# A gated recurrence with residual on one core: the order of the first loads, x of steps 8 to 15 by transposing load, and the last plain step by inner chunks

## The chip, the cores and the metric

The kernel runs on one core of a Trainium2 chip. The metric is the device time of one execution in microseconds, and the median of several runs is compared. A profile of one execution gives the times of the single instructions.

## What is computed

A GRU runs over 128 steps for a batch of 64. Input and state have 512 elements each. The kernel returns x plus the states of all steps, in float32:

```python
def step(h, inp):
    x_t, prop = inp
    comb = jnp.concatenate([x_t, h], axis=-1)
    z = jax.nn.sigmoid(comb @ Wz + bz)
    r = jax.nn.sigmoid(comb @ Wr + br)
    comb2 = jnp.concatenate([x_t, r * h], axis=-1)
    h_cand = jnp.tanh(comb2 @ Wh + bh)
    h_new = (1.0 - z) * h + z * h_cand
    h_next = jnp.where(prop, jnp.tanh(h_new @ Wp + bp), h_new)
    return (h_next, h_new)
```

`prop` is true at every fourth step, except at the last one. The upper 512 rows of each weight matrix meet x (tile `wx`, all three gates), the lower 512 meet the state (tiles `wh`). The recurrence is serial: a step's gates need the state of the step before. The part with x is known ahead and can be computed at any time before its step.

## The kernel before

**Layout.** The 512 columns are cut into two halves, and the 64 rows of the batch stand twice on the 128 partitions, once for each half. A product of one gate is four chunks of 128 input elements (k = 0 to 3, worked in the order 0, 2, 1, 3), each for both column halves: `product`, L195, one unit of the filler queue described below. The input of a product has to be transposed, with input elements on the partitions. `turn` (L204) does this on TensorE for the 16-bit words of the float32 values: four multiplies per 128 columns, and a copy out of PSUM.

**The parts with x.** Steps are taken in groups of four (g = t // 4). For steps 0 to 7 and for the last group they are plain products (`plain`, L410; `plain_last`): 12 units for a step, three gates times four chunks. All groups between go through `batch`: a nested scheme with seven products in place of eight at two levels, which needs sums of blocks of x (on POOL, `sum_raw12`, `sum_s12` and the like) and sums of blocks of `wx`. Part of the weight sums overwrite `wx` itself (`sum_outer_1`, L313, chunks 0 and 2; `sum_inner_1`, L322), so they come after the last plain product that reads those blocks, which is that of step 7.

**The order.** It is written out by hand; every engine works through its instructions in the order of the program. In a step TensorE does the R products from `hT`, the Z products, the turning of r*h, then filler units, the products of the candidate, filler units, and the turning of the new state. ACT does the sigmoids and tanh and part of the copies out of PSUM, DVE the elementwise work and other copies. `queue` holds the units of the parts with x, and `fill(n)` puts n of them where TensorE would wait for ACT and DVE. `read_out` appends the copies and sums that take a finished filler result out of PSUM; `seed` puts the x part of the next step into the accumulator, on ACT.

**x transposed.** There are two ways to it. `turn_x` (L235) turns one step's x on TensorE, with two copies on ACT: this is done for steps 0 to 15, from the tiles `xr` (groups 0 and 1) and `early` (groups 2 and 3). From group 4 on, `words_x` (L247, POOL) splits the words into a tile `xw`, `planes_x` (L257) issues a transposing load on SP from `xw` into `xv`, and `join_x` (L267, ACT) puts the words together in `xT`. `xw` and `xv` have one buffer each, `xT` two. The `early` tiles are two of the three buffers that later hold results of the batches (`mb`).

**The start.** SP asks for both halves of x of steps 0 and 1 (L109), then z's and the candidate's `wx`; ACT asks for r's `wx`, the initial state and three biases. Then SP goes on with the recurrent weights of r, x of steps 2 and 3, the bias of the propagation, the recurrent weights of z and of the candidate, and x of groups 1, 2 and 3 with `wp` between (L127 to L145). TensorE begins with multiplies of zeros (`idle`, L171, called from L595), turns x of steps 0 and 1 between them, and takes the plain products of steps 0 and 1 gate by gate before step 0 starts at L621.

Of the kernel before, what the change touches and what calls it, by code (L numbers as in the profile page):

```python
# [11 lines left out]
U16 = mybir.dt.uint16  # L12
# [5 lines left out]
def kernel(  # L18
# [29 lines left out]
    nc = tc.nc  # L48
    B, T, D = x.shape
    H = h0.shape[1]  # L50
    P = 128
    S = 2
    N = H // S
    C = N // P
    K = D // P
    Q4 = 4
    CHUNK = 4
    FIRST = 2
    LAST = T // Q4 - 1
    R, Z, H_ = range(3)  # L60
# [21 lines left out]
    wx = const.tile([P, K, 3, H], F32, name="wx")  # L82
# [5 lines left out]
    gates_in = (Wr, Wz, Wh)  # L88
    def load_x(tile_, t0, n, j=0):
        for s in range(S):  # L90
            nc.sync.dma_start(  # L91
                out=tile_[s * B : (s + 1) * B, j : j + n, :], in_=x[:, t0 : t0 + n, ts(s, N)]
            )

    def load_w(wt, w, k0, k1, eng):
        eng.dma_start(
            out=wt[:, k0:k1, :],
            in_=w[k0 * P : k1 * P, :].rearrange("(k p) n -> p k n", p=P),
        )

    xr = {}

    def new_xr(g):
        xr[g] = xrp.tile([P, Q4, N], F32, tag="xr", name=f"xr_{g}")
# [1 line left out]
    h_init = two.tile([P, N], F32, tag="h", name="h_init")  # L106
    bias_in = const.tile([P, 4, N], F32, name="bias")
    new_xr(0)
    load_x(xr[0], 0, 2)  # L109
    for i in range(3):  # L110
        for k in (0, 2):
            load_w(wx[:, :, i, :], gates_in[i], k, k + 2, nc.scalar if i == R else nc.sync)

    def load_bias(i, eng):
        for s in range(S):
# [22 lines left out]
    early = {}  # L138
# [25 lines left out]
    def cut(ps):  # L164
        return ps.rearrange("p (c n) -> p c n", c=C)
# [29 lines left out]
    def product(ps, lT, w, k, start=False):  # L195
        s0, c0 = divmod(k, C)
        products(ps, lT[:, c0, ts(s0, B)], lambda s: w[:, k, ts(s, N)], start)

    ORDER = [s * C + c for c in range(C) for s in range(S)]

    def copy(eng, dst, src):
        (eng.copy if eng is nc.scalar else eng.tensor_copy)(dst, src)  # L202

    def turn(src, dst, c, name, eng):  # L204


        pt = turn_ps[c][:, :P].bitcast(BF16).rearrange("p (w n) -> p w n", w=2)
        for s in range(S):
            words = src[:, c * P + s * B : c * P + (s + 1) * B].bitcast(BF16)
            for w in range(2):  # L210
                nc.tensor.transpose(  # L211
                    pt[s * B : (s + 1) * B, w, :],
                    words.rearrange("p (n w) -> p w n", w=2)[:, w, :],
                    ident16,
                )
        copy(
            eng,
            dst[:, c, :].bitcast(U16).rearrange("p (n w) -> p n w", w=2),
            pt.bitcast(U16).rearrange("p w n -> p n w"),
        )  # L220

    def new_T(tag, name):
        return two.tile([P, C, P], F32, tag=tag, name=name)
# [3 lines left out]
    xs = {}  # L227
    xw = {}
    xv = {}

    def new_xT(g):
        if g not in xT:
            xT[g] = xtp.tile([P, Q4, C, P], F32, tag="xT", name=f"xT_{g}")

    def turn_x(t, eng=nc.scalar):  # L235
        g, i = divmod(t, Q4)
        new_xT(g)
        src = xr[g] if g < 2 else early[g]
        for c in range(C):
            turn(src[:, i, :], xT[g][:, i], c, f"xT_{t}", eng)  # L240
# [6 lines left out]
    def words_x(g, i):  # L247

        if g * Q4 >= T:
            return  # L250
        if g not in xw:
            xw[g] = one.tile([P, Q4, 2, N], U16, tag="xw", name=f"xw_{g}")
        nc.gpsimd.tensor_copy(
            xw[g][:, i], xs[g][:, i, :].bitcast(U16).rearrange("p (n w) -> p w n", w=2)
        )

    def planes_x(g):  # L257

        if g * Q4 >= T:
            return  # L260
        xv[g] = one.tile([P, Q4, 2, C, P], U16, tag="xv", name=f"xv_{g}")
        nc.sync.dma_start_transpose(
            out=xv[g].rearrange("p t w c n -> p (t w c) n"),
            in_=xw[g].rearrange("p t w n -> p (t w n)"),
        )

    def join_x(g, i):  # L267

        if g * Q4 >= T:
            return  # L270
        new_xT(g)
        nc.scalar.copy(  # L272
            xT[g][:, i].bitcast(U16).rearrange("p c (n w) -> p w c n", w=2), xv[g][:, i]
        )


    def outer(kb, nb, ka):

        return wx[:, ka * C + kb, :, :].rearrange("p g (s n u) -> p n s g u", s=S, n=C)[:, nb]
# [12 lines left out]
    def inner(i, ka, na):  # L292
        return OPERAND[i](ka)[:, :, :, ts(na, P // 2)]
# [19 lines left out]
    def sum_outer_1():  # L313
        for ka in range(S):
            nc.vector.tensor_sub(outer(0, 1, ka), outer(0, 1, ka), outer(0, 0, ka))
# [6 lines left out]
    def sum_inner_1(i, eng):  # L322
        eng.tensor_sub(inner(i, 0, 1), inner(i, 0, 1), inner(i, 0, 0))
# [23 lines left out]
    def sum_s12(g):  # L347
        v = xT[g]
        o = sx[g, "o12"] = one.tile([P, 2, 2, P], F32, tag="o12", name=f"o12_{g}")
        nc.gpsimd.tensor_add(o[:, 0], v[:, 2:4, 0, :], v[:, 2:4, 1, :])  # L350
        nc.gpsimd.tensor_sub(o[:, 1], o[:, 0], v[:, 0:2, 0, :])
        s = sx[g, 56] = one.tile([P, 4, 2, B], F32, tag="s56", name=f"s56_{g}")
        four([s[:, n] for n in range(4)], o[:, :, 0], o[:, :, 1])
# [31 lines left out]
    def new_cp(q):  # L385
        if q not in cp:
            cp[q] = one.tile([P, C, 2, 3, P], F32, tag=f"cp{q % 2}", name=f"cp_{q}")
            for b in range(2):
                G[2 * q + b] = cp[q][:, :, b]

    def seed(i, t):
        if t < T:
            nc.scalar.copy(cut(slots[i]), G[t][:, :, i, :])  # L393
# [12 lines left out]
    def read_out():  # L406
        while pending:
            pending.pop(0)()

    def plain(t):  # L410

        first, second = scratch[:2] if t % 2 == 0 else scratch[2:]
        regions = (first[:, :N], first[:, N:], second[:, :N])
        g, i = divmod(t, Q4)

        def end():
            new_cp(t // 2)
            nc.vector.tensor_add(  # L418
                G[t][:, :, 0:2, :],
                first.rearrange("p (g c n) -> p c g n", g=2, c=C),  # L420
                bias[:, :, 0:2, :],
            )
            nc.vector.tensor_add(G[t][:, :, 2, :], cut(second[:, :N]), bias[:, :, 2, :])

        units = [
            lambda e=e, k=k: product(
                regions[e], xT[g][:, i], wx[:, :, e, :], k, k == ORDER[0] and e != Z
            )
            for e in range(3)
            for k in ORDER  # L430
        ]
        return [(u, None) for u in units[:-1]] + [(units[-1], end)]

# [187 lines left out]
    for t in range(T):  # L621
        g, j = divmod(t, Q4)
        prop = j == CHUNK - 1 and t < T - 1
        last = t == T - 1
        pair, u = divmod(t - 3, 8)
# [22 lines left out]
            assert len(queue) == 7  # L648

        def join(n):  # L650
            if pair >= 0 and u in (5, 6):
                join_x(even + 2, 2 * (u - 5) + n)
            elif pair >= 1 and u in (1, 3):
                join_x(odd, u - 1 + n)


        for k in ORDER:
            product(slots[R], hT, wh[R], k)
        if t < 6:
            turn_x((2, 5, 8, 11, 13, 15)[t])  # L660
        read_out()
        if u == 0 and pair >= 1 and odd - 2 < LAST:
            outer_u2(odd - 2)
        if t == 3:
            sum_s12(FIRST)
            for i in (1, 2, 3):
                sum_inner_1(i, nc.vector)
        rh = two.tile([P, N], F32, tag="rh", name=f"rh_{t}")
        for c in range(C):
            nc.scalar.activation(act_ps[c], slots[R][:, ts(c, P)], AF.Sigmoid)  # L670
# [30 lines left out]
        if t == 0:  # L701
            sum_outer()
            for i in (6, 7, 4):
                sum_inner(i, nc.gpsimd)
                sum_inner_1(i, nc.gpsimd)
        if not thin:
            fill(places[0])
        if t < 3:
            turn_x((3, 6, 9)[t])


        for k in ORDER:
# [12 lines left out]
            nc.vector.tensor_add(h_new[:, ts(c, P)], pc, keep[:, ts(c, P)])  # L725
        if t < T - 2:
            seed(H_, t + 1)
        read_out()
        fill(places[0] if thin else 5 if places[1] > 6 else 4)
        h = h_new  # L730
# [5 lines left out]
        fill(places[2] if thin else places[1] - 6)  # L736
        if t == 2:
            sum_outer_1()
        if prop:
            for k in ORDER:  # L740
                product(slot_p, hT, wp, k)
            read_out()
            h = two.tile([P, N], F32, tag="hprop", name=f"hprop_{t}")
            for c in range(C):
                nc.scalar.activation(h[:, ts(c, P)], slot_p[:, ts(c, P)], AF.Tanh)
            fill(behind[0] if thin else places[2] - 2)
            hT = new_T("hT", f"hpT_{t}")
            for c in range(C):
                turn(h, hT, c, f"hpT_{t}", (nc.vector, nc.scalar)[c])
            fill(behind[1] if thin else 2)  # L750
        if t < 5:
            turn_x((4, 7, 10, 12, 14)[t])


        if pair >= 0:
# [51 lines left out]
        n = 0  # L807
        if t >= T - CHUNK:
            n = {T - 2: 3, T - 1: 1}.get(t, 0)
        elif j == Q4 - 1:  # L810
            n = 4
        if n:
            for s in range(S):
                eng = nc.scalar if last and s else nc.sync
                eng.dma_start(
                    out=out[:, t - n + 1 : t + 1, ts(s, N)],
                    in_=xr[g][s * B : (s + 1) * B, j - n + 1 : j + 1, :],
# [52 lines left out]
```

## Time and profile before

| What | Value |
|---|---|
| Median of 3 runs | 1340.38 us (1339.74 to 1340.52) |
| The profiled execution: its own time, its span | 1341.68 us, 1339.9 us |
| TensorE matmul busy | 1326.0 us (99%) |
| TensorE weight load busy | 1109.8 us (83%) |
| DVE, ACT, POOL busy | 702.1 us (52%), 627.3 us (47%), 910.8 us (68%) |
| Moved by DMA | 76.74 MB, mean 57 GB/s |

The chain of work that ended last, followed back through the whole run, is 98% TensorE. By line it is L186, the products, with L211, the turning, at 5%. Busy time of an engine counts instructions that overlap, so a busy TensorE is not one at its peak. In the rows below, a group of instructions is named by line, engine and operation, and by the tile that it writes and those that it reads; "x8" is the number of instructions merged into a row. In square brackets stands the idle time of the engine before it and what ended it.

### The profile page before, as it was taken

What the parts mean: (1) busy time and instruction counts of PE and PEld (TensorE: products, weight loads), DVE (VectorE), ACT (ScalarE), POOL (GpSimd) and SP (SyncE); (2) the same over time, 40 slices, a digit from 0 to 9 for tenths busy, and PEclk for the clock granted to TensorE, in tenths of its full rate; (3) what the DMA queues carried; (4) which work ended last, traced back from release to release, by engine and by line L of the source; (5) the groups of instructions that cost most, each with busy time, mean ns of one, the idle gap of its engine ahead of it and who ended that gap; (6) DMA issues with size and microseconds to landing.
All of it is one profiled execution on the core that took longest, in us unless ns stands there. A gap on an engine that the chain in (4) does not pass through costs nothing.

```text
span 1339.9 us, 37622 instructions
## 1 busy us (share of the span) xinstructions
PE 1326.0 (99%) x15352; PEld 1109.8 (83%) x15352; DVE 702.1 (52%) x1867; ACT 627.3 (47%) x1851; POOL 910.8 (68%) x1110
## 2 busy tenths in 40 slices
PE   8999999999999999999999999999999999999998
PEld 5678888888888888888888888888888888888765
DVE  3355555555555555555555555555555555555444
ACT  1244545454554445445445544545445454554433
POOL 3448776787767777776787767777677777767500
PEclk8999999999999999999999999999999999999999
DMA  9211213122221212213212231223212222131210
GB/s 269 50 33 33 64 44 79 39 49 49 64 65 33 65 38 59 64 33 67 59 36 64 49 80 33 49 48 65 64 33 65 45 53 64 34 72 40 91 32 17
DMA packets 115500, 76.74 MB, mean 57 GB/s; under 512 B 61824, under 2 KB 110592, under 8 KB 115328
## 3 DMA queue, kind: packets, MB, share of 16 engines
q1 hardware_dynamic: 114064, 72.70, 23.5%
q8 instruction: 121, 1.98, 0.6%
q10 hardware_dynamic: 1264, 1.64, 0.5%
q14 instruction: 51, 0.42, 0.1%
HBM read 42.86 MB, written 16.78 MB: 45 GB/s over the span
## 4 chain that ended last, share of the span: by engine, by line
PE 98%; DMA 1%; DVE 0%; issue 0%; ACT 0%; SPq 0%; DVEq 0%; ACTq 0%
PE rc L186 33%; PE zp L186 20%; PE scratch_q L186 11%; PE scratch_r L186 11%; PE scratch_x L186 11%; PE scratch_a L186 6%; PE turn L211 5%; DMA xr<-in_x_dram 1%; ACT xT L202 0%; PE zp L174 0%; PE rc L174 0%; DVE turn L720 0%; SPq L91 0%; DVE h L725 0%; DVE xr L723 0%
## 5 line engine op out<-in xcount | busy, mean ns | idle before, releaser
L186 PE MATMUL rc<-wh,rhT 128*64 128x256 f32 x2048 | 245.9, 379 | 0.0
L186 PE MATMUL zp<-wh,hT 128*64 128x256 f32 x1536 | 204.3, 379 | 0.0
L186 PEld LDWEIGHTS rc<-wh,rhT 128*64 128x64 f32 x2048 | 167.6, 137 | 40.9
L542 POOL TENSOR_TENSOR cp<-mb,mb 128x768 f32<-128x768 f32 x72 | 130.9, 1818 | 102.1 <-ACT rc L393 54.5
L186 PE MATMUL rc<-wh,hT 128*64 128x256 f32 x1536 | 186.2, 383 | 0.3
L802 POOL TENSOR_TENSOR xr<-xr,h 128x256 f32<-128x256 f32 x127 | 92.8, 731 | 112.0 <-DVE h L725 111.0
L186 PEld LDWEIGHTS rc<-wh,hT 128*64 128x64 f32 x1536 | 121.1, 137 | 36.4 <-issue 9.7
L542 POOL TENSOR_TENSOR cp<-mb 128x768 f32<-128x768 f32 x44 | 79.9, 1817 | 99.3 <-ACT rc L393 98.1
L720 DVE TENSOR_TENSOR turn<-turn,z 128x128 f32<-128x128 f32 x256 | 75.4, 295 | 128.3 <-ACT turn L719 126.7
L186 PEld LDWEIGHTS zp<-wh,hT 128*64 128x64 f32 x1536 | 118.6, 137 | 25.0
L202 DVE COPY rhT<-turn 128x256 uint16<-128x256 uint16 x256 | 97.7, 420 | 69.9 <-PE turn L211 68.9
L670 ACT ACTIVATE turn<-rc 128x128 f32<-128x128 f32 x256 | 55.4, 261 | 163.2 <-issue 110.2
L202 ACT COPY hT<-turn 128x256 uint16<-128x256 uint16 x127 | 47.3, 373 | 168.6 <-DVE hT L202 128.0
L542 POOL TENSOR_TENSOR mb<-mb,mb 128x768 f32<-128x768 f32 x58 | 105.5, 1819 | 10.5 <-DVE mb L515 10.5
L393 ACT COPY rc<-cp 128x256 f32<-128x256 f32 x256 | 96.4, 376 | 19.5 <-DVE cp L418 8.0
L719 ACT ACTIVATE turn<-rc 128x128 f32<-128x128 f32 x256 | 55.2, 260 | 107.0 <-PE rc L186 105.9
L513 DVE TENSOR_TENSOR mb<-scratch_r,cq 128x384 f32<-128x384 f32 x102 | 56.7, 556 | 90.5 <-ACT cq L512 90.5
L506 DVE TENSOR_TENSOR cx<-scratch_r,cx 128x384 f32<-128x384 f32 x102 | 56.7, 556 | 86.8 <-ACT cx L504 86.8
L689 ACT ACTIVATE z<-zp 128x256 f32<-128x256 f32 x128 | 49.2, 384 | 95.3 <-PE zp L186 95.3
L272 ACT COPY xT<-xv 128x512 uint16<-128x512 uint16 x112 | 85.7, 765 | 0.0
L725 DVE TENSOR_TENSOR h<-turn,keep 128x128 f32<-128x128 f32 x254 | 74.1, 292 | 15.4
L211 PEld LDWEIGHTS <-h 128*64 128x64 bf16 x1016 | 67.9, 110 | 13.5 <-DVE h L725 6.4
(147 smaller groups left out, 3001.6 us busy)
## 6 DMA issues: line engine op xcount, KB each, us to landing
xr<-in_x_dram SPq DMA_DIRECT2D x62, 256.0 KB, 3.9
out_dram<-xr SPq DMA_DIRECT2D x62, 256.0 KB, 3.4
xs<-in_x_dram SPq DMA_DIRECT2D x56, 256.0 KB, 4.3
wx<-in_L_cond_Wr_dram ACTq DMA_DIRECT2D x2, 512.0 KB, 6.0
wx<-in_L_cond_Wz_dram SPq DMA_DIRECT2D x2, 512.0 KB, 9.5
wx<-in_L_cond_Wh_dram SPq DMA_DIRECT2D x2, 512.0 KB, 5.1
wh<-in_L_cond_Wr_dram SPq DMA_DIRECT2D x2, 512.0 KB, 5.6
wh<-in_L_cond_Wz_dram SPq DMA_DIRECT2D x2, 512.0 KB, 6.8
```

The lines of the kernel that those rows point to most:

```text
L186: nc.tensor.matmul(ps[s * B : (s + 1) * B], lhsT=lhs, rhs=rhs(s), start=start, stop=True, skip_group_check=True,)
L202: (eng.copy if eng is nc.scalar else eng.tensor_copy)(dst, src)
L211: nc.tensor.transpose(pt[s * B : (s + 1) * B, w, :], words.rearrange("p (n w) -> p w n", w=2)[:, w, :], ident16,)
L272: nc.scalar.copy(xT[g][:, i].bitcast(U16).rearrange("p c (n w) -> p w c n", w=2), xv[g][:, i])
L393: nc.scalar.copy(cut(slots[i]), G[t][:, :, i, :])
L506: nc.vector.tensor_add(T2[n][:, :nm], r_ps[:, :nm], T2[n][:, :nm])
L513: nc.vector.tensor_add(blocks()[:, :nm, 0, 1], r_ps[:, :nm], q2[:, :nm])
L542: nc.gpsimd.tensor_add(dst, a, b)
L670: nc.scalar.activation(act_ps[c], slots[R][:, ts(c, P)], AF.Sigmoid)
L720: nc.vector.tensor_mul(pc, pc, z[:, ts(c, P)])
L725: nc.vector.tensor_add(h_new[:, ts(c, P)], pc, keep[:, ts(c, P)])
L802: nc.gpsimd.tensor_add(xr[g][:, j, :], xr[g][:, j, :], h_new)
```

## The change

It has four parts.

- **Head of the queues.** The two halves of x of steps 0 and 1 go out on SP and on ACT, one each. The second half of r's `wx` stays on ACT, and the first half goes to SP, ahead of z's.
- **x of steps 8 to 15.** `turn_x` is called for steps 0 to 7 only. Groups 2 and 3 go by `words_x`, `planes_x` and `join_x`; their words are split on ACT, from the `early` tiles. The calls stand in steps 1 to 4. `turn_x(7)` moves from the end of step 1 to step 2, behind R.
- **The last plain step.** The units of step 7 are ordered by chunk, with the three gates of a chunk together.
- **Weight sums.** `sum_inner_1` of blocks 1 to 3 on DVE moves from step 3, behind the R products, to the end of step 2, right behind `sum_outer_1`.

```diff
-    load_x(xr[0], 0, 2)
+    for s in range(S):
+        (nc.sync, nc.scalar)[s].dma_start(
+            out=xr[0][s * B : (s + 1) * B, 0:2, :], in_=x[:, 0:2, ts(s, N)]
+        )
     for i in range(3):
         for k in (0, 2):
-            load_w(wx[:, :, i, :], gates_in[i], k, k + 2, nc.scalar if i == R else nc.sync)
+            load_w(
+                wx[:, :, i, :], gates_in[i], k, k + 2, nc.scalar if (i, k) == (R, 2) else nc.sync
+            )
...
-        nc.gpsimd.tensor_copy(
-            xw[g][:, i], xs[g][:, i, :].bitcast(U16).rearrange("p (n w) -> p w n", w=2)
+        src = (early if g < 4 else xs)[g]
+        copy(
+            nc.scalar if g < 4 else nc.gpsimd,
+            xw[g][:, i],
+            src[:, i, :].bitcast(U16).rearrange("p (n w) -> p w n", w=2),
         )
...
+        order = [(e, k) for e in range(3) for k in ORDER]
+        if t == FIRST * Q4 - 1:
+            order = [(e, k) for k in ORDER for e in range(3)]
         units = [
...
-            for e in range(3)
-            for k in ORDER
+            for e, k in order
         ]
...
         def join(n):
-            if pair >= 0 and u in (5, 6):
+            if t == 2 and n == 0:
+                join_x(2, 0)
+            elif t in (3, 4):
+                join_x(3, 2 * (t - 3) + n)
+            elif pair >= 0 and u in (5, 6):
...
-        if t < 6:
-            turn_x((2, 5, 8, 11, 13, 15)[t])
+        if t < 3:
+            turn_x((2, 5, 7)[t])
         read_out()
...
         if t == 3:
             sum_s12(FIRST)
-            for i in (1, 2, 3):
-                sum_inner_1(i, nc.vector)
...
+        if t == 1:
+            for n in range(4):
+                words_x(2, n)
+            planes_x(2)
+        elif t == 2:
+            for n in range(1, 4):
+                join_x(2, n)
+            for n in range(2):
+                words_x(3, n)
         if not thin:
             fill(places[0])
-        if t < 3:
-            turn_x((3, 6, 9)[t])
+        if t < 2:
+            turn_x((3, 6)[t])
...
         if t < T - 2:
             seed(H_, t + 1)
+        if t == 2:
+            for n in range(2, 4):
+                words_x(3, n)
+            planes_x(3)
         read_out()
...
         if t == 2:
             sum_outer_1()
+            for i in (1, 2, 3):
+                sum_inner_1(i, nc.vector)
...
-        if t < 5:
-            turn_x((4, 7, 10, 12, 14)[t])
+        if t == 0:
+            turn_x(4)
```

## The prediction

> **What bounds the kernel now.** I read the page first, then TensorE's own list of waits, then the start in order of time beside the windows and the landings of the loads. The page gives TensorE 1326.0 of 1339.9 us. Its list of waits, longest first, is short (who waited for whom: total us, times, longest):
>
> ```profile
> PE turn L211 <- DMA xr<-in_x_dram: 4.5, 1, 4.5
> PE turn L211 <- DVE rh L671: 2.4, 2, 1.4
> PE rc L174 <- DVE zeros L73: 1.2, 1, 1.2
> PE turn L211 <- DVE h L725: 0.2, 1, 0.2
> ```
>
> So there are three things to win: work taken off TensorE, the 4.5 us at the start, and 2.4 us of waiting for rh. Whatever moves between the other engines costs nothing until it makes TensorE wait. The start, in order of time (start us, length, engine, line):
>
> ```profile
> 4.18 0.44 PE L174 MATMUL zp<-zeros 128*64 128x512 bf16 x2
> ...
> 9.10 0.64 PE L211 MATMUL turn<-ident,xr 128*64 128x128 bf16 x8 [4.48 <-DMA xr<-in_x_dram]
> ...
> 12.48 2.93 PE L186 MATMUL scratch_q<-wx,xT 128*64 128x256 f32 x16
> ...
> 17.80 1.10 SPq L96 DMA_DIRECT2D wh<-in_L_cond_Wz_dram  x2
> ...
> 26.04 1.48 PE L186 MATMUL zp<-wh,hT_init 128*64 128x256 f32 x12
> ```
>
> The idle multiplies with zeros end at 4.62, x lands at 8.96, products start at 12.48 and at half clock: a set of 16 takes 1.73 us later on and 2.68 us here, about 1 us lost. The third line tells when z's recurrent weights are asked for, the last when step 0 uses them. Now the windows of the same stretch (busy us of PE, PEld, DVE, ACT, POOL, then granted clock, DMA share, GB/s), and the landing of z's two halves (KB each, median us):
>
> ```profile
> 8.00:9.00 1.00, 0.00 (x0) 0.00 (x0) 0.00 (x0) 0.00 (x0) 0.00 (x0) 0.50 1.05 248
> ...
> 16.00:20.00 4.00, 4.00 (x42) 2.85 (x40) 0.00 (x0) 0.00 (x0) 3.36 (x4) 1.00 1.07 368
> ...
> 2.00:25.60 23.60, 19.12 (x161) 12.40 (x159) 4.31 (x10) 2.54 (x5) 8.73 (x9) 0.86 1.03 299
> ...
> wh<-in_L_cond_Wz_dram SPq DMA_DIRECT2D x2, 512.0 KB, 6.8
> ```
>
> From 2 to 25.6 us the DMA engines are full: share 1.03, 299 GB/s. The first half of z's wh lands 6.4 us after its issue, so the second, issued at 18.4, takes 7.2: it lands at 25.6, and step 0 starts on it at 26.04 (queued from 25.99). After the wait for x, then, the kernel runs only some 0.5 us behind its loads.
>
> **Part 1, the head of the queues.** x goes out as one half on SP and one on ACT, ahead of everything; r's weights follow, one half on each. Before, x's halves took 5.5 and 7.4 us beside r's megabyte. Alone at the head of two queues they are near the 256 KB x loads of steady running (3.9 us): about 0.8 + 3.9, so 4.7, just when the zeros end. R's halves landed at 5.8 and 8.1; they still need x's 256 KB and their own 1 MB moved, so about 7.9. Products start near 7.9 in place of 12.3.
>
> Here a rule speaks against taking that as the gain. The waits and the half clock say 4.5 + 1.0 = 5.5 us. The Trainium skill ("DMA: Bandwidth & Descriptors", section "Issuing engines are not separate DMA queues") says that DMAs from different engines run on the same 16 DMA engines and interleave, so that a second issuer saves only issue time. By the rule what counts is how many bytes stand ahead of each deadline. Up to z's second half these are x 0.26, the three wx 3.15, h 0.13, biases 0.52, r's wh 1.05, x of steps 2 and 3 0.26, z's wh 1.05 MB: 6.4 MB before and 6.4 MB after, through engines that are full in both. I take the rule, as the windows carry it, and lay TensorE's new schedule over the landings:
> - r products 7.9 to 11.4 (two sets of 1.73). z's wx landed at 13.2; with 0.27 MB of bias and of the next load ahead of it moved back, about 12.7: wait 1.3.
> - z products to 16.2, turning h 0.2; the candidate's wx landed at 17.4, its second half having been asked for only at 13.3 behind a wait. Earlier issue, about 17.0: wait 0.7. Products to 20.5.
> - step 0: R 1.73 (r's wh landed at 20.4), a turn 0.22: ready for Z at 22.4. z's wh landed at 25.6 before. With nothing lost it could be 23.5: an estimate at 368 GB/s for weights (16 to 20 us) and some 190 for x and biases (25 to 35 us at about 270, where a good third is x) gives 21.5 us from 2.0 on. The windows show the engines full, so I stay near the old landing and take 25.0, for the earlier requests. Z starts there in place of 26.2: **gain 1.2 us** (0.6 if it lands as before, 2.6 at best).
> - the candidate's wh landed at 29.6 for its last half; needed at 25.0 + 7.3 = 32.3. No further wait. That 7.3 is the distance from Z at 26.22 to the H products at 33.5.
>
> **Part 2, x of steps 8 to 15.** Eight calls of turn_x go: 64 multiplies on TensorE and 16 ACT copies. One call, between R and Z, seen by the starts:
>
> ```profile
> 59.39 0.39 PE L211 MATMUL turn<-ident,early 128*64 128x128 bf16 x8
> ...
> 59.61 1.47 PE L186 MATMUL zp<-wh,hT 128*64 128x256 f32 x12
> ```
>
> 59.61 - 59.39 = 0.22 us each; 8 x 0.22 = **1.76 us** off the engine that sets the end. In their place come 8 ACT copies of words, two transposing loads on SP, and 8 ACT joins:
>
> ```profile
> L272 ACT COPY xT<-xv 128x512 uint16<-128x512 uint16 x112 | 85.7, 765 | 0.0
> ...
> DMA to landing us min/median/max: 4.2/4.3/6.2
> ```
>
> A join is 0.765 us. The copy of words stands in the trace on POOL only (0.62); on ACT the nearest row is the join, same size and kind, so 0.77, between 0.62 and twice a 256-wide turn copy's 0.37. ACT takes 16 x 0.77 = 12.3 us and gives back 8 x 0.65 = 5.2. Where it lies: step 1, four copies behind seed(Z), 46.6 to 49.7, then tanh at 52.3; the early tile landed at 34.7. Step 2, join at 61.1, then z, 1-z, seed, three joins and two copies to 67.3; tanh at 69.1, or 68.7 with two turns gone; two more copies 69.5 to 71.1, then the ACT half of hT, due at 71.4. Nothing waits. SP issues a transposing load in 1.8 us; its next duty behind is the store at 90.1. Cost 0; were the cover gone in step 2, some 0.5 us.
>
> The landings: group 2's load leaves at 49.7 and lands at 54, used at 61. Group 3's leaves at 71.1, lands at 75.4, and join(3, 0), the first ACT work behind seed(R) of step 3, comes at 76.9. These are the tight 1.5 us. A late join does not block rh, which is ahead of it; it holds up z and tanh, and from there hT.
>
> **Part 3, the rh waits.** They are in steps 4 and 5, beside a turn_x both times. Step 4:
>
> ```profile
> 91.83 0.65 ACT L202 COPY xT<-turn 128x256 uint16<-128x256 uint16 x2 [1.31 <-PE turn L211]
> 92.36 0.50 ACT L504 COPY cx<-scratch_x 128x384 f32<-128x384 f32 x1
> 92.73 0.51 ACT L505 COPY cq<-scratch_q 128x384 f32<-128x384 f32 x1
> ...
> 93.10 0.48 ACT L670 ACTIVATE turn<-rc 128x128 f32<-128x128 f32 x2
> ...
> 94.17 0.50 PE L211 MATMUL turn<-ident,rh 128*64 128x128 bf16 x8 [0.98 <-DVE rh L671]
> ```
>
> The x copy, which waits for its turn behind R, stands on ACT ahead of cx and cq, and they ahead of the sigmoid. scratch_q is done near 89.7, so without the turn both run during R and the sigmoid is next. In step 5 it is the copy cq of L512, at 102.52 behind an x copy, and three adds of DVE behind it ahead of rh: 1.43 us at 104.79; its scratch_q is done near 98. Later steps do the same work without a turn, and TensorE records no such wait. **2.4 us** gone. Were only step 4's to go, 1.0.
>
> **Part 4, the last plain step and the sums.** The k order keeps step 7's 12 units (one gate, one input chunk). sum_outer_1 needs chunks 0 and 2 (now done after unit 6 of 12, before after 10), the three sums on DVE chunk 1 (after 9). They take 1.83 + 1.49 us: 71.9 to 75.2, then the 1.1 us of bias adds that wait for the last unit, to 76.3; the sigmoid of step 3 ends about then, and TensorE asks for rh after Z at 77.2. The same DVE work stood before rh earlier, with the end at 77.31. Gain 0, as TensorE did not wait there; it lets the earlier sigmoid through.
>
> **Sum.** 1.2 + 1.76 + 2.4 = 5.4 us. Span 1339.9 to 1334.5. The profiled run took 1341.68, 1.3 over the median of the runs, 1340.38; I take the difference from the median: **1335.0**.
>
> **Rivals.**
> - Loads do not bind. For: x is the only DMA wait that TensorE records. Against: share 1.03 to 25.6 us. Gain 5.5 + 4.2 = 9.7: 1330.7.
> - The clock falls in the new waits. The clock dropped once, at 7.85, 3.2 us into the idle stretch from 4.62, and was back at 14.27, 5.2 us after work resumed: half of it lost is 2.6 us. The new wait ahead of Z is 2.6 us long, behind waits of 1.3 and 0.7. The Trainium skill ("TensorE: Matmul & The Clock Gate", "Why this matters for your kernels") sets the bound at gaps of about 3 us; by the row 2.6 is safe too, but by little, if z's weights land late. Gain 5.4 - 2.6 = 2.8: 1337.6.
> - Slower: the transposing loads land late. Group 3: ACT's work from join(3, 0) to tanh is 3.8 us (the second join, 0.77; four copies and sigmoids, 1.5; cx and cq, 1.0; a hop by DVE, 0.5), and tanh is due at 83.0, so the load may land at 78.4, 7.3 us after its issue. Group 2: 6.2 us of ACT work to a tanh due at 68.7 leave until 62.4, 12.7 us after issue. Each us beyond costs one. At 13 us group 3 loses 5.7 and the gain is gone; loads in the full queue took up to 14.3 (early, issued at 25.6), which loses 7.0 + 1.6: 3.2 us slower, 1343.6. Against: 28 such loads landed within 6.2 us, and DMA is nearly idle from 45 to 90 us.
> - z's weights land as before (0.6 less) and the copies eat 0.5 us: within the likeliest case.
>
> **Chances.** Likeliest case 0.65, its own range 1333.6 to 1336.6; loads not binding 0.10; clock 0.15; slower 0.10. A difference under 0.2% (2.7 us) cannot be told from none. The clock case lies on that bound and is halved; a tenth of the slower case ends inside it, as does a little of the likeliest. Faster 0.64 + 0.10 + 0.07 = 0.81; same 0.01 + 0.08 + 0.01 = 0.10; slower 0.09. The range goes from 1332.0, most of the way to the second case, to 1338.5, just past the third.
>
> **What would show it.** TensorE's wait for x near 0; in its place waits at L186 for wx and, above all, for z's wh just ahead of step 0's Z, which should start at 25.0 +- 0.7; granted clock 1.00 from about 8 us on. Rows of turn<-ident,early gone. No wait for rh left. Words on ACT near 0.77 us. I am wrong if Z of step 0 starts before 23.5 (loads did not bind) or not before 26 us, or if steps 1 to 5 show TensorE waiting for h or rh.

## The result, and the profile after

| | Before | After |
|---|---|---|
| Median, runs of the same chip | 1340.29 us (6 runs, 1339.66 to 1341.37) | 1335.47 us (6 runs, 1334.57 to 1337.85) |
| Profiled execution: its time, its span | 1341.68, 1339.9 us | 1337.25, 1335.4 us |
| TensorE matmul busy | 1326.0 us | 1324.3 us |

The ratio is 0.9967, with a 95% interval of 0.9955 to 0.998: 4.8 us less by the medians, 4.5 by the two spans. The forecast, 1335.0, was 0.5 us off. That closeness is in part luck: the total hides errors of more than 1 us that cancel.

TensorE's list of waits after the change (who waited for whom: total us, times, longest):

```profile
PE zp L191 <- DMA wh<-in_L_cond_Wz_dram: 1.7, 2, 1.0
PE scratch_q L191 <- DMA wx<-in_L_cond_Wr_dram: 1.6, 1, 1.6
...
PE turn L216 <- DVE rh L684: 0.5, 2, 0.3
PE rc L191 <- DMA wh<-in_L_cond_Wr_dram: 0.5, 1, 0.5
```

The 4.5 us wait for x is gone, and in its place stand 3.8 us of waits for weights. The rh waits are 0.5 in place of 2.4 us. L216 and L191 are the old L211 and L186. The start, in order of time (start us, length, engine, line):

```profile
4.60 0.64 PE L216 MATMUL turn<-ident,xr 128*64 128x128 bf16 x8
...
8.65 1.95 PE L191 MATMUL scratch_q<-wx,xT 128*64 128x256 f32 x16 [1.59 <-DMA wx<-in_L_cond_Wr_dram]
...
23.48 0.65 PE L191 MATMUL zp<-wh,hT_init 128*64 128x256 f32 x4 [1.02 <-DMA wh<-in_L_cond_Wz_dram]
24.85 1.17 PE L191 MATMUL zp<-wh,hT_init 128*64 128x256 f32 x8 [0.71 <-DMA wh<-in_L_cond_Wz_dram]
...
33.50 1.90 PE L191 MATMUL rc<-wh,rhT 128*64 128x256 f32 x16
```

x is turned at 4.60, the products start at 8.65 (before: 12.48), and Z begins chunk by chunk at 23.48 and 24.85 (before: 26.04). Yet the candidate's products of step 0 start at 33.50, and before they started at 33.51. The windows say where the lead went (busy us of PE, PEld, DVE, ACT, POOL, then granted clock, DMA share, GB/s), with the landing of z's recurrent weights below:

```profile
11.00:12.00 1.00, 1.00 (x14) 0.64 (x11) 0.00 (x0) 0.99 (x2) 0.00 (x0) 1.00 0.54 155
...
23.00:24.00 1.00, 0.52 (x4) 0.20 (x4) 0.49 (x2) 0.76 (x4) 0.92 (x2) 1.00 1.06 389
24.00:25.00 1.00, 0.29 (x4) 0.15 (x4) 0.00 (x0) 0.00 (x0) 0.96 (x1) 1.00 1.05 387
...
26.00:27.00 1.00, 1.00 (x14) 0.71 (x10) 0.73 (x2) 0.00 (x0) 0.04 (x1) 0.50 1.13 217
...
2.00:25.60 23.60, 19.76 (x182) 11.43 (x180) 4.80 (x12) 3.90 (x10) 9.46 (x10) 1.00 0.99 318
```

```profile
wh<-in_L_cond_Wz_dram SPq DMA_DIRECT2D x2, 512.0 KB, 8.0
```

To 25.6 us the DMA engines are again full on average (share 0.99), with a hole at 11 to 13 us. TensorE is half idle from 22 to 25 us, and then the granted clock is 0.50 until about 29 us. Weights asked for earlier took longer to land (8.0 against 6.8 us).

Starts of the same work on TensorE in both profiled executions show where the 4.5 us come from:

| Start of | Before | After | Gained so far |
|---|---|---|---|
| candidate's products, step 0 | 33.51 | 33.50 | 0.0 |
| R, step 3 | 74.44 | 74.07 | 0.4 |
| turning of rh, step 3 | 77.70 | 77.60 | 0.1 |
| R, step 4 | 89.77 | 89.43 | 0.3 |
| turning of rh, step 4 | 94.17 | 92.45 | 1.7 |
| R, step 5 | 99.91 | 97.69 | 2.2 |
| turning of rh, step 5 | 104.79 | 100.73 | 4.1 |
| candidate's products, last step | 1332.85 | 1328.50 | 4.4 |

The largest steps are at rh in steps 4 and 5, which now comes without a wait. Step 4 after the change:

```profile
89.43 1.90 PE L191 MATMUL rc<-wh,hpT 128*64 128x256 f32 x16
...
92.45 0.39 PE L216 MATMUL turn<-ident,rh 128*64 128x128 bf16 x8
```

Two questions follow: is the start worth nothing, or did the half clock of this execution eat it? And what is lost in steps 2 and 3?

### The profile page after: what moved, and what is told of

Same layout as the page of the kernel before. It is cut to its first block, busy times and chain, and to the rows that moved or that the text cites. A ratio compares the mean times of both kernels' runs of the same rounds, so it can differ in the third digit from the quotient of the medians.

```text
span 1335.4 us, 37500 instructions
## 1 busy us (share of the span) xinstructions
PE 1324.3 (99%) x15288; PEld 1108.0 (83%) x15288; DVE 703.1 (53%) x1867; ACT 631.9 (47%) x1851; POOL 910.1 (68%) x1110
## 4 chain that ended last, share of the span: by engine, by line
PE 97%; DMA 2%; DVE 1%; issue 0%; SPq 0%; ACT 0%; DVEq 0%; ACTq 0%
PE rc L191 33%; PE zp L191 20%; PE scratch_q L191 11%; PE scratch_r L191 11%; PE scratch_x L191 10%; PE scratch_a L191 6%; PE turn L216 5%; DMA wh<-in_L_cond_Wz_dram 1%; DMA wx<-in_L_cond_Wz_dram 1%; DMA wx<-in_L_cond_Wh_dram 0%; DVE wx L323 0%; DVE wx L331 0%; DVE turn L742 0%; DVE cp L426 0%; SPq L96 0%
## 5 line engine op out<-in xcount | busy, mean ns | idle before, releaser
L191 PE MATMUL rc<-wh,rhT 128*64 128x256 f32 x2048 | 246.0, 379 | 0.0
L191 PE MATMUL zp<-wh,hT 128*64 128x256 f32 x1536 | 204.4, 379 | 0.0
L191 PEld LDWEIGHTS rc<-wh,rhT 128*64 128x64 f32 x2048 | 168.0, 137 | 40.8
L191 PE MATMUL rc<-wh,hT 128*64 128x256 f32 x1536 | 186.2, 383 | 0.2
L191 PEld LDWEIGHTS rc<-wh,hT 128*64 128x64 f32 x1536 | 121.3, 137 | 36.7 <-issue 9.5
L191 PEld LDWEIGHTS zp<-wh,hT 128*64 128x64 f32 x1536 | 118.9, 137 | 25.2
L280 ACT COPY xT<-xv 128x512 uint16<-128x512 uint16 x120 | 91.7, 766 | 0.0
L216 PEld LDWEIGHTS <-h 128*64 128x64 bf16 x1016 | 68.0, 110 | 13.5 <-DVE h L747 6.4
```

Of the source, the lines that this page charges most:

```text
L191: nc.tensor.matmul(ps[s * B : (s + 1) * B], lhsT=lhs, rhs=rhs(s), start=start, stop=True, skip_group_check=True,)
L216: nc.tensor.transpose(pt[s * B : (s + 1) * B, w, :], words.rearrange("p (n w) -> p w n", w=2)[:, w, :], ident16,)
L280: nc.scalar.copy(xT[g][:, i].bitcast(U16).rearrange("p c (n w) -> p w c n", w=2), xv[g][:, i])
```

## The experiments

Each edit is against the changed kernel unless it says otherwise. "Before" in each is the kernel before on the same chip.

**1. The old head, all else changed.**

```diff
-    for s in range(S):
-        (nc.sync, nc.scalar)[s].dma_start(...)
+    load_x(xr[0], 0, 2)
...
-            load_w(..., nc.scalar if (i, k) == (R, 2) else nc.sync)
+            load_w(..., nc.scalar if i == R else nc.sync)
```

> The changed kernel with the head of the queues as before (parts 2 to 4 alone). Theory, the loads bind and the clock falls in the new waits: the head's share of the median is small, so parts 2 to 4 give nearly all: 1.8 us of turns, 2.8 us of rh waits (by the spacing of the starts) and 0.5 us around the turn at the end of step 4, less 0.8 us of new rh waits in steps 2 and 3. 4.3 us under the kernel before, some 1336.0, with the small spread of the kernel before. Rival, the head gives most of the gain: 1338 or more. The rh waits of steps 2 and 3 should stand in its trace as in the changed kernel.

Measured: 1336.21 us (5 runs, 1336.08 to 1336.73) beside 1340.93; ratio 0.9967 (0.9955 to 0.998). Without the new head the gain is 4.7 us, as large as with it (4.8). The granted clock is 1.00 throughout its start. Its start, in order of time:

```profile
11.92 2.23 PE L186 MATMUL scratch_q<-wx,xT 128*64 128x256 f32 x16
...
24.78 1.48 PE L186 MATMUL zp<-wh,hT_init 128*64 128x256 f32 x12
...
32.26 1.90 PE L186 MATMUL rc<-wh,rhT 128*64 128x256 f32 x16
```

With the old head Z can start at 24.78, not only at 26.04 as in the profile of before. The 1.26 us between are 0.56 by which x landed later there (products at 12.48 against 11.92) and 0.70 by which the first set ran longer there, at half clock (2.93 against 2.23).

**2. Zeros in the waits for z's weights**, to hold the clock. They go to a scratch tile and enter no result.

```diff
+        if t == 0:
+            idle_q(8)
-        for k in ORDER[: 2 if thin else 3]:
+        for n, k in enumerate(ORDER[: 2 if thin else 3]):
             product(slots[Z], hT, wh[Z], k)
+            if t == 0 and n == 0:
+                idle_q(6)
```

> The changed kernel with multiplies of zeros in the two waits ahead of step 0's Z products (eight before the first chunk, six behind it); they compute nothing that is used. Theory, the clock falls because TensorE is about half idle from 22.4 to 25 us: the granted clock stays at 1.00 behind 25 us, step 0's H products start near 32 us in place of 33.5, the median falls by 1 to 1.6 us to 1334 or below and the spread shrinks. Rival, the drop comes from the waits further ahead (7 to 8.6 us and 20 to 20.7) or costs nothing: the clock still drops, or the time stays at 1335.5.

Measured: 1335.45 us (1334.88 to 1337.47); 0.9963 (0.9949 to 0.9976). The profiled execution has the clock at 1.00 behind 25 us and the candidate's products at 32.34. The median is not lower by what can be told. The spread did not shrink either (2.6 us), and its run of 1337.47 has a mean clock of 1.0, so the clock is not the only cause of the spread.

**3. Real filler units in the same waits**: `fill(3)` ahead of Z and `fill(2)` behind its first chunk, five fewer later in step 0.

> The changed kernel with five of step 0's twelve filler units moved into the two waits ahead of and between its Z products. Theory, the waits are lost time and cost the clock as well: 1.7 us of waits filled and the clock kept at 1.00, so 2 to 3.3 us under the changed kernel, 1332.2 to 1333.5. Rival, Z comes later by the filler and the rest of the step waits for z and tanh: TensorE waits at the turn of h, and the time is 1335 or more.

Measured: 1336.83 us (6 runs, 1336.12 to 1337.77); 0.997 (0.9959 to 0.9982). The rival's case: the turning of rh, between Z's products, began only at 28.57 us (26.29 in experiment 6), and the five units missing later in the step became a wait for h. TensorE's list has 1.5 us of it in two pieces, of which one of 0.2 stands in the changed kernel too.

**4. POOL's sums of group 2 behind rh of step 3.**

```diff
-        if t == 3:
-            sum_s12(FIRST)
...
             nc.vector.tensor_mul(rh[:, ts(c, P)], act_ps[c], h[:, ts(c, P)])
+        if t == 3:
+            nc.gpsimd.tensor_copy(mark, rh[0:1, N - 1 : N])
+            sum_s12(FIRST)
```

> The changed kernel with POOL's sums of group 2 held back until rh of step 3 is there. Theory, DVE's weight sums at the end of step 2 are slowed by POOL working at the same time: the two rows of sum_outer_1 go from 2.59 back to 1.85 us, the three of sum_inner_1 from 2.27 to 1.5, and the wait for rh in step 3 (0.34 us by the list, 0.5 by the starts) is gone. Rival, the sums are slow because of where they stand or what they wait for in TensorE's order: the rows stay long and the wait stays.

First the changed kernel in step 3, in order of time. The sums of x run on POOL beside the sums of weights on DVE, and TensorE waits:

```profile
71.28 0.73 POOL L358 TENSOR_TENSOR o<-xT 128x256 f32<-128x256 f32 x1
71.64 2.59 DVE L323 TENSOR_TENSOR wx<-wx 128x768 f32<-128x768 f32 x2
...
73.49 1.05 POOL L340 TENSOR_TENSOR s<-o 128x128 f32<-128x128 f32 x1
...
74.15 2.27 DVE L331 TENSOR_TENSOR wx<-wx 128x384 f32<-128x384 f32 x3
...
77.60 0.51 PE L216 MATMUL turn<-ident,rh 128*64 128x128 bf16 x8 [0.34 <-DVE rh L684]
```

Then the kernel with POOL's sums later, the same two DVE rows:

```profile
70.28 1.82 DVE L323 TENSOR_TENSOR wx<-wx 128x768 f32<-128x768 f32 x2
...
72.02 1.49 DVE L331 TENSOR_TENSOR wx<-wx 128x384 f32<-128x384 f32 x3
```

The kernel before has the same sums of weights (its L315 and L323) at this speed, and POOL begins only when they are over:

```profile
73.14 1.83 DVE L315 TENSOR_TENSOR wx<-wx 128x768 f32<-128x768 f32 x2 [1.27 <-PE scratch_x L186]
...
75.82 1.49 DVE L323 TENSOR_TENSOR wx<-wx 128x384 f32<-128x384 f32 x3
...
77.23 0.73 POOL L350 TENSOR_TENSOR o<-xT 128x256 f32<-128x256 f32 x1 [5.75 <-ACT xT L202]
...
78.84 0.46 POOL L332 TENSOR_TENSOR s<-o 128x128 f32<-128x128 f32 x1
```

With POOL later, 4.86 us of sums become 3.31, and from the start of R to the turning of rh it takes 3.03 in place of 3.53 us. The list keeps 0.2 us of rh, in step 2. The single run took 1336.83 us, which for half a microsecond tells nothing. The trace does: the 0.5 us in step 3 come from POOL's and DVE's sums meeting.

**5. The new head alone, in the kernel before.** The edit is the first part of the change.

> The kernel before with the new head of the queues alone. Theory, z's recurrent weights set step 0's Z under either head: that product starts near 24.5 to 25 us and the time is the kernel before's or up to 0.7 us less, 1340.0 to 1340.9; in the trace TensorE's wait for x is gone and waits for weights stand in its place, of the same sum. Rival, the wait for x (4.5 us) and the half clock after it are won: 1336 to 1338.

Measured: 1340.68 us (13 runs, 1339.86 to 1342.09) beside 1340.51 (18 runs); **1.0 (0.9992 to 1.0009)**. No gain can be told, and by the interval it is at most 1.1 us.

**6. The changed kernel again**, on the same chip.

> The changed kernel once more, for a comparison on one chip with the two others of this call: 1335.5, of which the difference to the kernel with the head alone, 4 to 5 us, is what parts 2 to 4 give. In its trace the clock may or may not fall behind 25 us; if the fall costs 1.4 us in step 0, its span shows it, by the start of step 0's H products near 32.1 or 33.5.

Measured: 1336.28 us (6 runs, 1335.34 to 1337.59); 0.9969 (0.9958 to 0.9981). All but the head is worth 4.4 us. The two starts, the head alone first and then the changed kernel, each with its window from 26 to 27 us:

```profile
24.77 1.97 PE L191 MATMUL zp<-wh,hT_init 128*64 128x256 f32 x8 [0.71 <-DMA wh<-in_L_cond_Wz_dram]
...
33.42 1.90 PE L191 MATMUL rc<-wh,rhT 128*64 128x256 f32 x16
...
26.00:27.00 1.00, 1.00 (x14) 0.67 (x12) 0.01 (x1) 0.00 (x0) 0.00 (x0) 0.50 1.15 230
```

```profile
25.38 1.08 PE L191 MATMUL zp<-wh,hT_init 128*64 128x256 f32 x8 [0.72 <-DMA wh<-in_L_cond_Wz_dram]
...
32.35 1.90 PE L191 MATMUL rc<-wh,rhT 128*64 128x256 f32 x16
...
26.00:27.00 1.00, 1.00 (x20) 0.68 (x17) 0.38 (x2) 0.00 (x0) 0.08 (x1) 1.00 1.15 217
```

The first has a stretch of half clock from about 24.8 to 28.2 us, the second none. From the first product on the second half of z's weights to the candidate's products it is 8.65 us in the first (and 8.65 in the profile after), 6.97 in the second: the drop, some 3.4 us long, costs 1.7 us where it happens. At full clock all the way, the candidate's products start at 32.35, 32.13 and 32.17 with the new head (experiments 6, 4, 8) and at 32.26 with the old (experiment 1). So the new head gains nothing at step 0 even where the clock holds.

**7. z's second half of `wx` on ACT, and POOL's sums later.** In the changed kernel SP's request for the candidate's first half waits until z's first half has landed (6.0 us in SP's list of waits), though it needs nothing of it. A completion semaphore that both loads share would explain this; no run shows it.

```diff
-                ..., nc.scalar if (i, k) == (R, 2) else nc.sync
+                ..., nc.scalar if (i, k) in ((R, 2), (Z, 2)) else nc.sync
```

> The changed kernel with the second half of z's wx asked for by ACT, and POOL's sums of group 2 held back until rh of step 3. Theory: in the changed kernel the load of the candidate's wx was asked for only at 10.45 us, behind a wait, and DMA fell to 155 GB/s from 11 to 13 us; with z's half on ACT the candidate's first half is asked for at once, the hole is gone, and z's recurrent weights land about 1 us sooner: step 0's H products near 31.2 us. With 0.5 us from step 3 that is 1.5 us under the changed kernel, some 1334. Rival, the hole only moves, as the same bytes stand ahead: H products at 32.1, and 0.5 us in all.

Measured: 1335.40 us (1334.6 to 1339.05); 0.9966 (0.9954 to 0.9979). The candidate's first half now leaves at 2.92 us, but its second half waits for r's load, to 9.21, and r's recurrent weights wait in turn, to 13.07. So the hole moves, to 13 to 15 us. The requests in the changed kernel, and the second half here:

```profile
10.45 0.95 SPq L96 DMA_DIRECT2D wx<-in_L_cond_Wh_dram  x2
```

```profile
9.21 0.37 SPq L96 DMA_DIRECT2D wx<-in_L_cond_Wh_dram  x1
```

The candidate's products start at 31.02, 1.33 us before experiment 6. The wait in step 3 is gone again. The median is 0.9 us under experiment 6, within the spread of both.

**8. Part 4 undone**: step 7's units by gate, and the sums of blocks 1 to 3 behind the R products of step 3.

> The changed kernel with part 4 undone: step 7 by gates, the three sums back in step 3. Theory: POOL's sums of group 2 now run early, beside DVE's, so the sums behind the R products end later and rh of step 3 waits 1 us or more in place of 0.34. Rival, part 4 does nothing for the time: the wait stays at 0.3 to 0.4.

The single run took 1337.45 us. In step 3:

```profile
74.84 2.71 DVE L331 TENSOR_TENSOR wx<-wx 128x384 f32<-128x384 f32 x3
...
77.81 0.51 PE L216 MATMUL turn<-ident,rh 128*64 128x128 bf16 x8 [1.86 <-DVE rh L684]
```

R started at 72.75, so rh's turn comes 5.06 us behind it, against 3.53 with part 4. In these two traces part 4 saves 1.5 us of step 3, once part 2 has POOL's sums run early.

**9. The kernel before, with two copies of x moved**: the turns of x of steps 13 and 15 are written behind the sigmoids of steps 4 and 5, so that their copies stand behind these on ACT.

```diff
-        if t < 6:
-            turn_x((2, 5, 8, 11, 13, 15)[t])
+        if t < 4:
+            turn_x((2, 5, 8, 11)[t])
...
+        if t in (4, 5):
+            turn_x((13, 15)[t - 4])
         seed(R, t + 1)
```

> The kernel before, with turn_x(13) and turn_x(15) written behind the sigmoids of steps 4 and 5 in place of ahead of them. No turn is taken out, TensorE's work and order are the same. Theory, the rh waits of these steps come from ACT's order alone (the copies of x ahead of cx, cq and the sigmoids): both waits are gone from the list and the time falls by what their spacing says, 2.8 us, to 1337.7; the part of the change's gain that needs no transposing load. Rival, the waits come with the turns themselves or with the sums of DVE: they stay, wholly or in part, and the time stays within 1 us of the kernel before.

Measured: 1339.61 us (21 runs, 1338.26 to 1340.96) beside 1340.9 (26 runs); 0.999 (0.9984 to 0.9997): 1.3 us of the 2.8 expected. The trace in step 4:

```profile
91.41 0.50 PE L211 MATMUL turn<-ident,early 128*64 128x128 bf16 x8 [0.75 <-DVE rh L671]
```

rh is begun 2.30 us behind the start of R (4.06 before). The order on ACT was the cause of the late rh. But the turn of x writes the PSUM tile that rh still reads, so it waits 0.75 us (0.83 in step 5) in front of Z. Of the three versions only the one without the turn has neither delay: R to the turning of rh takes 4.40 and 4.88 us in the kernel before, 4.25 and 4.36 here, 3.02 and 3.04 after the change. Here that is 0.7 us less than before in all, and the median's 1.3 agrees with it within its interval. A turn written behind that of rh was not tried in these steps.

**10. Fewer bytes ahead of z's recurrent weights**: x of steps 2 and 3 goes behind them, the bias of the propagation behind the candidate's, and `turn_x(2)` behind the turning of rh.

> The changed kernel with x of steps 2 and 3 and the propagation's bias (0.39 MB) asked for behind z's recurrent weights, and the turn of step 2 behind rh's turn. Theory, the bytes ahead of z's recurrent weights set the start: 0.39 MB at the 190 to 370 GB/s of this stretch is 1 to 2 us, so step 0's Z product starts near 22.5 and the H products near 31 us in place of 32.3, 1.3 us less in all: 1334.2 to 1335. Rival, another wait takes its place (the recurrent weights of r, or x of step 2 arriving too late for the filler): H products at 32 us or later, no gain.

Measured: 1336.43 us (6 runs, 1335.21 to 1337.92) beside 1340.9; 0.997 (0.9958 to 0.9982). In the trace:

```profile
23.40 1.08 PE L191 MATMUL zp<-wh,hT_init 128*64 128x256 f32 x8 [1.28 <-DMA wh<-in_L_cond_Wz_dram]
...
31.40 1.93 PE L191 MATMUL rc<-wh,rhT 128*64 128x256 f32 x16
```

The second half is there 2.0 us and the candidate's products start 0.95 us before experiment 6. In this trace, then, the bytes ahead set that landing. The median does not show the microsecond.

**11. Experiments 7 and 10 together.**

> All of the last tries together on the changed kernel: z's half on ACT, x of steps 2 and 3 and the propagation's bias behind z's recurrent weights, POOL's sums behind rh of step 3. Theory: H products of step 0 near 30 us in place of 32.3, 0.5 us from step 3, so some 2.5 us under the changed kernel, 1333.5 or less on a chip on which that takes 1336. Rival, the start then waits for the candidate's recurrent weights or the clock falls in the waits that are left: 1335 or more.

Measured: 1335.08 us (5 runs, 1334.16 to 1337.6); 0.9962 (0.9949 to 0.9974). This is the lowest median and, beside the changed kernel's 1335.47 and 1336.28, not told from it. Its profiled execution had a stretch of half clock again, with the candidate's products at 34.20.

## Why the prediction held, point by point

- **Part 1, 1.2 us: wrong, no gain was measured.** The landing was right: the second half's products began at 24.85 for a forecast 25.0, and experiments 5 and 6 give 24.77 and 25.38. The waits before it fell elsewhere (1.6 for r's `wx` and 0.5 for r's `wh`, not 1.3 and 0.7 for z's and the candidate's `wx`), which changes nothing behind that landing. The failed term is the 26.2 that it was subtracted from. The prediction took Z's start from the chain view of one execution (the row that it shows has 26.04), in which x came 0.56 us later and the clock was half for 0.70 us more than in experiment 1. It named the half clock as "about 1 us lost" and still let it into the gain, although that execution lay 1.3 us above its median. Experiments 1 and 5, from both sides, find no gain of the head; experiment 5 leaves room for 1.1 us at most. So the rule on issuing engines held more fully than the prediction dared to use it: with 6.4 MB ahead of the deadline under either head, what the head takes from the wait for x it gives back in waits for weights. The count of bytes is not all, though: in experiment 7 the same bytes stand ahead, and the second half was there 1.3 us sooner than in experiment 6 (24.04 against 25.38), in one trace each. The case of loads that do not bind (1330.7) is refuted by the same runs.
- **Part 2, 1.76 us: right.** The table of starts closes with 0.22 for each turn: up to R of step 3 three turns are gone and 0.31 is lost to rh in step 2, so 0.35 (0.37 in the table); up to rh's turn one more, less the 0.49 of step 3, so 0.08 (0.10 from the starts); up to R of step 4 one more, 0.30 (0.34). Words on ACT cost less than the 0.77 assumed, 0.61 us each, and overlap a little: one row shows four in 2.17 us:

```profile
46.56 2.17 ACT L207 COPY xw<-early 128x512 uint16<-128x512 uint16 x4
```

  The transposing loads were never late: group 3's join began at 76.84 without a wait for its load, against 76.9 worked out. The slower rival did not occur.
- **Part 3, 2.4 us: right in kind, too small.** The waits of steps 4 and 5 are gone. By the spacing of R and rh's turn, with the turn of x between them (0.22) taken off, step 4 gave 4.40 - 0.22 - 3.02 = 1.16 and step 5 gave 4.88 - 0.22 - 3.04 = 1.62, together 2.8. The list's 0.98 and 1.43 are lower; the profile models the ends of matmuls. Experiment 9 confirms the order on ACT as the cause of the late rh.
- **Missed: a new wait of 0.5 us in step 3.** "No wait for rh left" was wrong. The prediction followed where the earlier x sets ACT and TensorE to work, and not where it sets POOL: the cost of that was put at nothing without a reason. Group 2's x is ready sooner, so POOL's sums, which began at 77.23 as DVE's ended (77.31), now begin at 71.28 and run beside them. The Trainium skill ("SBUF — State Buffer", section "SBUF: two separate sides") says that a DVE instruction with both inputs in SBUF and a GpSimd instruction that reads SBUF exclude each other for a whole instruction. The rows agree: the two DVE rows grew by 0.76 and 0.78, about one POOL instruction each (0.73), and POOL's own row from 0.46 to 1.05. In step 2 another 0.2 to 0.3 us of rh are lost: the second of DVE's two multiplies starts late, at 60.84 and not right behind the first (60.33). This does not come from the earlier x. It stands in experiment 5 as well, which has the new head alone, and is missing in experiment 1, which has all but the head, and also in 2 and 10; what splits the two multiplies stays open.
- **Part 4, 0: wrong beside part 2.** It was put at nothing because TensorE did not wait there before. With part 2's earlier sums on POOL it saves 1.5 us of step 3 (experiment 8).
- **The clock rival: half true.** The clock does fall behind the new waits, in three of the eight profiled executions that have the new head and nothing put into its waits (after, 5 and 11), and costs 1.7 us rather than 2.6. Zeros in the waits kept it up in the one trace and did not lower the median.
- **Its own signs.** By two of them it would have been wrong: TensorE waits for rh in steps 2 and 3, and Z's first chunk began at 23.48, just ahead of the 23.5 named as the limit. The second is no sign of loads that do not bind, as the second half came at 24.85. A third, a clock of 1.00 from 8 us on, failed in the profile after.
- **Readings that were off without weight in the sum.** The best case of 23.5 comes to about 22.5 by the rates it names (5.24 MB at 368 GB/s and 1.18 MB at 190 are 20.5 us). The clock fell at 7.7 and was back at 14.5, not at 7.85 and 14.27: a window's 0.85 or 0.73 is a mean of 1.00 and 0.50.

The errors cancel so: 1.2 too much for the head, some 0.8 for the new rh waits (0.5, and 0.3 in step 2), against 0.4 too little for part 3, 0.3 more than a turn's 0.22 between rh's turn in step 4 and R of step 5 (x's turn took 0.42 us there, from 99.49 to 99.91, and rh's 0.33 in place of 0.23), and 0.3 after rh's turn of step 5 that no run traces to its cause. So 5.4 becomes 4.4, where the last products stand.

**Open.** The changed kernel spreads over 3.3 us in 6 runs, experiment 1 with the old head over 0.65 in 5, but the kernel before, with the same old head, over 2.4 in 26 (experiment 9). Whether the new head widens the spread is therefore not shown. The clock explains a part at most: run 1337.47 of experiment 2 had it full. The gains of 1 us at step 0 in experiments 7 and 10 are plain in the traces and lost in that spread.

## What to carry to other kernels

A wait for the first load is not a gain until the bytes ahead of the next deadlines have been counted: where the DMA engines are full, another order moves the wait. A gain read from the start of one execution must be measured from an execution with the same granted clock. And when work is moved forward, look at what it wakes: here the earlier x set POOL going beside DVE, and the edit that was put at nothing kept the harm at 0.5 us in place of 2.

## What was not expected of the hardware

- The clock fell to half at about 25.7 us behind waits of at most 1.02 us, with TensorE 0.47, 0.52 and 0.29 busy from 22 to 25 us. The Trainium skill ("TensorE: Matmul & The Clock Gate", "Why this matters for your kernels") warns of gaps of about 3 us, and no gap here is that long. In experiment 6, with waits of 0.91 and 0.72, it stayed at 1.00. The length of a gap alone does not tell. The busy share comes nearer: its lowest value over any 3 us after 18 us was 0.42, 0.36 and 0.39 in the three executions in which the clock fell (after, 5, 11), and 0.43 to 0.53 in the five in which it stayed (4, 6, 7, 8, 10). These lie too close together to make a rule.
- A DMA request can wait for the landing of an earlier load of which it needs nothing. The candidate's first half left only at 10.45 us, 6.0 us after its turn in SP's queue, and moved bytes fell to 155 GB/s at 11 to 13 us with work still queued behind it. With one of z's requests moved to the other queue it left at 2.92, and the requests behind it waited in its place. That a shared completion semaphore is the reason is not shown.
